# Two graph-attention layers on one core: the dense products beside the edge sums traced in four column pieces, and a bias added by VectorE

## The chip, the cores and the metric

The kernel runs on one NeuronCore of a Trainium2 chip. The metric is the device time of one execution in microseconds (us). TensorE (PE) multiplies matrices, VectorE (DVE) and ScalarE (ACT) work element by element, GpSimd (POOL) writes the descriptors of the gathers, SyncE (SP) issues most plain transfers, and 16 DMA engines move the data between the device memory and the core's SBUF. PSUM is the memory into which TensorE writes.

## The reference, cut to what matters

A graph has 3125 nodes of 768 features and 53125 edges, sorted by destination, self-loops among them. The node table passes a norm and a ReLU, then two attention layers, and `x` is added at the end:

```python
def gat_conv(x, edge_index, W, a_src, a_dst, bias, heads, out_ch, concat):
    ...
    xl = (x @ W).reshape(n, heads, out_ch)
    ...
    alpha = e / (s[dst] + 1e-16)
    msg = xl[src] * alpha[:, :, None]
    out = jax.ops.segment_sum(msg, dst, num_segments=n)
    ...
h = gat_conv(x, edge_index, W1, a_src1, a_dst1, b1, HEADS, HID, True)
h = layer_norm(h, g1, be1)
h = jax.nn.relu(h)
h = h + (h0 @ Wr1 + br1)
h1 = h
h = gat_conv(h, edge_index, W2, a_src2, a_dst2, b2, 1, OUT_DIM, False)
h = layer_norm(h, g2, be2)
h = h + (h1 @ Wr2 + br2)
```

Layer 1 has 4 heads of 256 columns (1024 in all), layer 2 one head of 768. Everything is in 32-bit floats. The dense products of the change are `h0 @ Wr1` (its late part), `h1 @ W2` and `h1 @ Wr2`.

## The kernel before, in words

The nodes are cut into 25 blocks of 128 (the last has 53). The edges of a block are laid out in 17 tiles of 128 slots (8 in the last block), so that a tile's edges lead to one or two quarters of the block, 32 nodes each. The function `in_order` does all the work; `any_order` is for other inputs and does not run here.

**Before the sums.** Up to about 503 us the kernel computes the norm, the table of layer 1 (`x @ W1`), the edge lists, the attention weights of layer 1, and `h0 @ Wr1` for about half of the blocks.

**The sums of layer 1** (`sums`, L639, called at L1184). For every block there are five rounds (`ROUNDS`) of three or four tiles. For each tile, GpSimd issues an indirect DMA (L698) that gathers 128 rows of 1024 floats of the table by the edges' sources into one of 13 buffers `g`. VectorE makes the weights `w` (L718, L719). TensorE then adds the products (L738): each takes 32 weight columns, one quarter's nodes, and writes 32 partitions of PSUM, so that four of them cover the four quarters of a block. After each round `step` lets the other work of TensorE advance, in an order that is written out by hand: the ends of earlier blocks, and `later`, which computes the late part of `h0 @ Wr1` (L1101) at the pace of the tuple `(2.5, 3.8, 0, 0, 0.9)` per round. The end of a block (`end1`, L1129) normalizes the sum, turns it by TensorE transposes (L1151), adds the residual (L1158, VectorE, both sources in SBUF), and multiplies by `W2` (L1173) to make a row block of layer 2's table, `table2`. That table must be whole before the first gather of layer 2.

**The sums of layer 2** (from L1187). The scheme is the same with rows of 784 floats and 36 buffers for the gathers (`RING`, issued by `fetch`, L1280). For each block, ScalarE copies the edge values (L1300), TensorE turns them (L1318), VectorE and ScalarE form the softmax (L1321 to L1328), TensorE turns the result back (L1332), and then come five rounds of sums (L1354). After each round, `filled` advances `residuals` (L1249), which computes `h1 @ Wr2` (L1259) some three blocks ahead: one of eight steps of K after each of the first four rounds, and four steps after the fifth. In round 2 the transposes L1318 stand between the sums and the product, in round 4 the transposes L1332. VectorE ends a block with L1367 (reads PSUM), L1370, the norm's statistics (L480, L482), L1373 and L1374.

**The biases `br2` and `be2`.** `split_biases` (L200) adds them, divides the sum into two rounded parts and stores them. `bias_rows` (L214) loads these as two rows. At the last step of K, two products of a row of ones with them (L1263) add them into PSUM:

```python
for k in range(NK2):
    for i, pm in enumerate(pms):
        nc.tensor.matmul(pm[:, :f], h1[:, k, :r], wr2[:, k, i * f:(i + 1) * f],
                         start=(k == 0), stop=False)
    if k == NK2 - 1:
        for i, pm in enumerate(pms):
            nc.tensor.matmul(pm[:, :f], ones_r[:, :r], ball_r[:, i * f:(i + 1) * f],
                             start=False, stop=True)
    yield
```

VectorE then adds the result to `xr`, a block of `x` (L1268). One 32-bit product in the program gives two matmul instructions and two weight loads in the trace.

Of the kernel before, what the change touches and what calls it, by code (L numbers as in the profile page):

```python
# [10 lines left out]
F32 = mybir.dt.float32  # L11
F32R = mybir.dt.float32r
# [5 lines left out]
OP = mybir.AluOpType  # L18
# [50 lines left out]
def in_order(  # L69
# [69 lines left out]
    hot_d = dram.tile([NB, 128, WIN], F8, name="hot_d")  # L139
    parts_d = dram.tile([2, C2], F32, name="parts_d")  # L140

# [3 lines left out]
    nc.vector.tensor_copy(ident_b, ident)  # L145
    ones_r = const.tile([2, P], F32R, name="ones_r")
    nc.vector.tensor_scalar(ones_r, ident[0:2, :P], 0.0, 1.0, op0=OP.mult, op1=OP.add)
    eps = const.tile([128, 1], F32, name="eps")
# [28 lines left out]
    def bcast(vec, n, parts=P):  # L177
        return bass.AP(tensor=vec.tensor, offset=vec.offset, ap=[[0, parts], [1, n]])

    def pieces(b):  # L180
        n = rows_of(b)
        m = n - n % 16
        return [(0, m), (m, n)] if m < n else [(0, n)]
# [15 lines left out]

    def split_biases(pool):  # L200

# [4 lines left out]
        nc.vector.tensor_add(v, v, u)  # L206
        hi = pool.tile([128, C2 // 128], F32R, name="ball_hi")
        nc.vector.tensor_copy(hi, v)
        lo = pool.tile([128, C2 // 128], F32R, name="ball_lo")
        nc.vector.tensor_sub(lo, v, hi.bitcast(F32))  # L210
        for i, t in enumerate((hi, lo)):
            nc.sync.dma_start(parts_d[i, :].rearrange("(p c) -> p c", p=128), t.bitcast(F32))

    def bias_rows(pool, name):  # L214
        t = pool.tile([2, C2], F32R, name=name)
        nc.sync.dma_start(t.bitcast(F32), parts_d)
        return t

# [535 lines left out]
    with tc.tile_pool(name="m1", bufs=1) as mp:  # L754
# [8 lines left out]
        with tc.tile_pool(name="h0", bufs=1) as hp, tc.tile_pool(name="pm1", bufs=1, space=PSUM) as pm1, \  # L763
# [9 lines left out]
            with tc.tile_pool(name="w1", bufs=1) as wp, tc.tile_pool(name="d1", bufs=2) as dp, \  # L773
# [216 lines left out]
                fill = early()  # L990
                split_biases(mp)
                for _ in products_:
# [82 lines left out]
        with tc.tile_pool(name="w2", bufs=1, reuse_waits="tile") as wp, tc.tile_pool(name="e1", bufs=2, reuse_waits="tile") as ep, \  # L1075
# [14 lines left out]
            def later():  # L1090
                for i, members in enumerate(late_in):
# [6 lines left out]
                    for m in range(NK2):  # L1098
                        pm = pp.tile([128, 512], F32, name="pr", bufs=2)
                        for k in range(NK1):  # L1100
                            nc.tensor.matmul(pm[:, :n], wr1[:, k, m * 128:(m + 1) * 128], loaded[i, k][:, :n],  # L1101
                                             start=(k == 0), stop=(k == NK1 - 1))
                            if m == NK2 - 1:
# [25 lines left out]
            def end1(b, z, share):  # L1129
# [41 lines left out]
                for k in range(NK2):  # L1171
                    for pm, (o, n) in zip(pms, halves):
                        nc.tensor.matmul(pm[:, :n], hT[:, k, :r], w2[:, k, o:o + n],  # L1173
                                         start=(k == 0), stop=(k == NK2 - 1))
                    if k in (2, 5, 7):
                        yield
# [10 lines left out]
    with tc.tile_pool(name="m2", bufs=1, reuse_waits="tile") as mp, \  # L1187
# [13 lines left out]
        for t in slots:  # L1201
            nc.vector.memset(t, 0.0)
        ball_r = bias_rows(mp, "ball_r")
        nc.vector.tensor_tensor(both, asad2[:, :, 0], asad2[:, :, 1], OP.add)
# [39 lines left out]
        owns = {0: small([128, C2], "own")}  # L1244
        z0 = small([P, C2], "z", bufs=2)
        nc.sync.dma_start(b2_b, bcast(b2, C2))
        nc.sync.dma_start(g2_b, bcast(g2, C2))

        def residuals():  # L1249

            for b in range(NB):
# [5 lines left out]
                for k in range(NK2):  # L1257
                    for i, pm in enumerate(pms):
                        nc.tensor.matmul(pm[:, :f], h1[:, k, :r], wr2[:, k, i * f:(i + 1) * f],  # L1259
                                         start=(k == 0), stop=False)  # L1260
                    if k == NK2 - 1:
                        for i, pm in enumerate(pms):
                            nc.tensor.matmul(pm[:, :f], ones_r[:, :r], ball_r[:, i * f:(i + 1) * f],  # L1263
                                             start=False, stop=True)
                    yield
# [635 lines left out]
```

## Time and profile before

| What | Value |
|---|---|
| Time, median of 3 runs | 1811.11 us (1810.21 to 1814.62) |
| The profiled execution's own time | 1811.92 us |
| Its span, first to last instruction | 1810.0 us |
| Mean granted TensorE clock | 0.974 |
| Busy: PE, DVE, ACT, POOL | 1691.0, 974.1, 452.4, 882.0 us |
| Gathers of layer 1 (L698), of layer 2 (L1287) | 416 and 416 |
| First and last sum of layer 1 (L738) | 503.5 and 1190.3 us |
| First and last gather issue of layer 2 | 1225.5 and 1775.6 us |

Times inside the trace count from the start of the span. "Busy" is the union of an engine's instructions. A row of a view that groups instructions gives the line, the engine, the operation, its output and inputs, the shape, how many there were, their busy time and the mean of one in ns, and the idle time just before them with what ended it. "DMA share" is the busy share of the 16 DMA engines, in which overlapping packets count twice, so that it can pass 1.

### The profile page before, as it was taken

The numbers are of one execution on the slowest core, as the hardware profiler recorded it, in microseconds if no ns is written. First come the engines' busy times: TensorE is split into PE (matmuls) and PEld (weight loads), VectorE is DVE, ScalarE is ACT, GpSimd is POOL, SyncE is SP. The second block draws the span as 40 slices with busy tenths as digits, with TensorE's granted clock in tenths as the row PEclk, the third lists the DMA queues.
The fourth block names the chain that finished last, engine by engine and source line by source line (L and its number), as shares of the span: only waits on it lengthen the run. The fifth ranks groups of instructions, "written<-read, shape, count | busy, mean of one in ns | idle before, by whom it ended". The sixth has DMA issues, their size and how long they took to land. (4 is left out here: it accounts for less than half of the span.)

```text
span 1810.0 us, 30659 instructions
## 1 busy us (share of the span) xinstructions
PE 1691.0 (93%) x11397; PEld 945.2 (52%) x11397; DVE 974.1 (54%) x2617; ACT 452.4 (25%) x1286; POOL 882.0 (49%) x922
## 2 busy tenths in 40 slices
PE   7999999899968999999999999996989999899995
PEld 5666665566535656566565455543434444344432
DVE  7683443788855465655656664631334444344445
ACT  2222331000121222122122112122333333343333
POOL 2000112000056566666666665606777777777772
PEclk9999999999988999999999999998999999999997
DMA  7834546533199999999999999939999999999994
GB/s 237 274 104 144 137 123 203 219 120 122 36 366 408 365 401 393 389 407 381 404 410 402 411 398 372 385 128 358 343 381 383 395 386 372 380 390 392 377 358 152
DMA packets 173674, 561.37 MB, mean 310 GB/s; under 512 B 28740, under 2 KB 54106, under 8 KB 173388
## 3 DMA queue, kind: packets, MB, share of 16 engines
q0 software_dynamic: 100912, 402.06, 58.2%
q1 hardware_dynamic: 68210, 146.87, 22.7%
q10 hardware_dynamic: 4394, 10.39, 1.5%
q8 instruction: 93, 1.52, 0.3%
q14 instruction: 65, 0.53, 0.1%
HBM read 498.23 MB, written 65.62 MB: 312 GB/s over the span
## 5 line engine op out<-in xcount | busy, mean ns | idle before, releaser
L698 POOL DMA_INDIRECT g<-table,idx_s x416 | 408.0, 981 | 418.1 <-DVE m L619 175.5
L1287 POOL DMA_INDIRECT g<-table,idx_s x416 | 417.8, 1004 | 179.5 <-issue 62.3
L1259 PE MATMUL pr<-wr,h 128*128 128x384 f32 (+1 forms) x800 | 293.1, 508 | 0.0
L738 PE MATMUL pa<-g,w 128*32 128x256 f32 x3912 | 261.0, 390 | 23.6 <-DMA g<-table,idx_s 12.5
L1173 PE MATMUL p<-w,h1T 128*128 128x384 f32 (+2 forms) x800 | 279.8, 498 | 2.6 <-DVE h1T L1158 2.6
L1259 PEld LDWEIGHTS pr<-wr,h 128*128 128x128 f32 (+1 forms) x800 | 145.0, 193 | 123.5 <-issue 53.3
L1173 PEld LDWEIGHTS p<-w,h1T 128*128 128x128 f32 (+1 forms) x800 | 144.9, 188 | 122.2 <-issue 25.2
L738 PEld LDWEIGHTS pa<-g,w 128*32 128x32 f32 x3912 | 125.2, 111 | 152.4 <-issue 30.1
L1354 PE MATMUL pa<-g,w 128*32 128x384 f32 x1956 | 192.7, 507 | 3.1 <-DVE v L1379 3.1
L719 DVE TENSOR_TENSOR w<-oh,al 128x128 f32<-128x128 f32 (+1 forms) x416 | 131.9, 317 | 91.3 <-PE pa L738 57.0
L1321 DVE CUSTOM_DVE_ANT_0 e<-mix,pen 128x640 f32<-128x640 f32 x25 | 20.6, 825 | 235.1 <-PE mix L1318 235.1
L1101 PE MATMUL pr<-h0k,wr 128*128 128x256 f32 (+1 forms) x576 | 141.0, 392 | 0.0
L843 PE MATMUL pm<-w,h0l 128*128 128x344 f32 (+1 forms) x468 | 140.8, 455 | 0.0
L980 PE MATMUL pm<-h0g,wr 128*128 128x512 f32 x288 | 132.0, 606 | 0.0
L843 PE MATMUL pm<-w,h0g 128*128 128x344 f32 x432 | 130.8, 459 | 0.3 <-ACT h0g L822 0.3
L1300 ACT ACTIVATE slots<-g 128x32 f32<-128x32 f32 x416 | 73.7, 221 | 221.7 <-DMA g<-table,idx_s 221.6
L1101 PEld LDWEIGHTS pr<-h0k,wr 128*128 128x128 f32 x576 | 106.9, 191 | 29.4 <-issue 9.0
L911 POOL DMA_DIRECT2D hot_d<-ohd x25 | 13.4, 537 | 219.0 <-DVE own L497 121.5
L1354 PEld LDWEIGHTS pa<-g,w 128*32 128x32 f32 x1956 | 54.5, 112 | 117.7 <-issue 91.4
L718 DVE TENSOR_SCALAR oh<-iota_f,rel_s 128x32 f32<-128x32 f32 (+1 forms) x416 | 110.1, 265 | 0.1
L843 PEld LDWEIGHTS pm<-w,h0l 128*128 128x128 f32 (+1 forms) x468 | 84.9, 186 | 44.0 <-issue 5.7
L843 PEld LDWEIGHTS pm<-w,h0g 128*128 128x128 f32 x432 | 82.0, 193 | 40.6 <-issue 1.6
(286 smaller groups left out, 1640.7 us busy)
## 6 DMA issues: line engine op xcount, KB each, us to landing
s<-slo_d SPq DMA_DIRECT2D x25, 544.0 KB
g<-table,idx_s POOLq DMA_INDIRECT x832
table<-row SPq DMA_DIRECT2D x24, 512.0 KB
own<-table SPq DMA_DIRECT2D x24, 512.0 KB
h1T_d<-h1T SPq DMA_DIRECT2D x24, 512.0 KB
h<-h1T_d SPq DMA_DIRECT2D x22, 512.0 KB
table<-row SPq DMA_DIRECT2D x24, 392.0 KB
ring<-in_x_dram SPq DMA_DIRECT2D x24, 384.0 KB
```

Source lines behind the costliest of these rows:

```text
L698: nc.gpsimd.indirect_dma_start(out=g, out_offset=None, in_=table[:, :], in_offset=bass.IndirectOffsetOnAxis(ap=idx_s[:, b * J + j:b * J + ...
L718: nc.vector.tensor_scalar(oh, iota_f[:, lo:hi], rel_s[:, c:c + 1], None, op0=OP.is_equal)
L719: nc.vector.tensor_tensor(w, oh[:, None, :].to_broadcast([128, heads, hi - lo]), al[:, POS[j], :, b:b + 1].to_broadcast([128, heads, hi - ...
L738: nc.tensor.matmul(pa[32 * q:32 * q + 32, o // f, o % f:o % f + n], w[:, o // cols, :], g[:, o:o + n], start=to not in opened, stop=False, ...
L843: nc.tensor.matmul(pm[:r, :C], h0[b][:, k, :], w1[:, k, i * C:(i + 1) * C], start=(k == 0), stop=(k == NK1 - 1))
L980: nc.tensor.matmul(pm, wr1[:, k, m * 128:(m + 1) * 128], groups[gi][:, k, :], start=(k == 0), stop=(k == NK1 - 1))
L1101: nc.tensor.matmul(pm[:, :n], wr1[:, k, m * 128:(m + 1) * 128], loaded[i, k][:, :n], start=(k == 0), stop=(k == NK1 - 1))
L1173: nc.tensor.matmul(pm[:, :n], hT[:, k, :r], w2[:, k, o:o + n], start=(k == 0), stop=(k == NK2 - 1))
L1259: nc.tensor.matmul(pm[:, :f], h1[:, k, :r], wr2[:, k, i * f:(i + 1) * f], start=(k == 0), stop=False)
L1287: nc.gpsimd.indirect_dma_start(out=g, out_offset=None, in_=table2[:, :], in_offset=bass.IndirectOffsetOnAxis(ap=idx_s[:, b * J + j:b * J + ...
L1300: nc.scalar.activation(slots[b % 2][:, POS[j], :], gs[b, j][:, C2:C2 + 1].to_broadcast([128, 32]), AF.Copy)
L1354: nc.tensor.matmul(pa[32 * q:32 * q + 32, i, :f], w_, g[:, i * f:(i + 1) * f], start=(i, q) not in opened, stop=False, skip_group_check=True)
```

## The change

A helper `by_columns` splits a product's weights into pieces of at most 32 columns, each with the PSUM partitions of its own. The three dense products that run beside the sums (L1101, L1173, L1259) go through it, so that each becomes four products of 32 weight columns over the same moving data. The row of ones, the two rounded parts and the two products L1263 go. In their place `br2 + be2` is stored whole, loaded once into all 128 partitions (`ball_b`, by SP, just ahead of `b2_b`), and VectorE adds it to each block's `xr` at step 5 of K.

```diff
--- before.py
+++ after.py
@@ -137,14 +137,12 @@
     slo16_d = dram.tile([NB * S], I16, name="slo16_d")
     keep_d = dram.tile([H * NB, S + 2], BF16, name="keep_d")
     hot_d = dram.tile([NB, 128, WIN], F8, name="hot_d")
-    parts_d = dram.tile([2, C2], F32, name="parts_d")
+    ball_d = dram.tile([C2], F32, name="ball_d")
 
     ident = const.tile([128, 128], F32, name="ident")
     make_identity(nc, ident)
     ident_b = const.tile([128, 128], BF16, name="ident_b")
     nc.vector.tensor_copy(ident_b, ident)
-    ones_r = const.tile([2, P], F32R, name="ones_r")
-    nc.vector.tensor_scalar(ones_r, ident[0:2, :P], 0.0, 1.0, op0=OP.mult, op1=OP.add)
     eps = const.tile([128, 1], F32, name="eps")
     nc.vector.memset(eps, EPS)
     iota_i = const.tile([128, 128], I32, name="iota_i")
@@ -177,6 +175,12 @@
     def bcast(vec, n, parts=P):
         return bass.AP(tensor=vec.tensor, offset=vec.offset, ap=[[0, parts], [1, n]])
 
+    def by_columns(out_, lhsT, rhs, m, start, stop):
+
+        for o in range(0, m, 32):
+            e = min(o + 32, m)
+            nc.tensor.matmul(out_[o:e], lhsT[:, o:e], rhs, start=start, stop=stop, skip_group_check=True)
+
     def pieces(b):
         n = rows_of(b)
         m = n - n % 16
@@ -197,24 +201,14 @@
         nc.sync.dma_start(t, vec.rearrange("(k p) -> p k", p=128))
         return t
 
-    def split_biases(pool):
+    def sum_biases(pool):
 
         v = pool.tile([128, C2 // 128], F32, name="ball_v")
         nc.sync.dma_start(v, br2.rearrange("(p c) -> p c", p=128))
         u = pool.tile([128, C2 // 128], F32, name="ball_u")
         nc.sync.dma_start(u, be2.rearrange("(p c) -> p c", p=128))
         nc.vector.tensor_add(v, v, u)
-        hi = pool.tile([128, C2 // 128], F32R, name="ball_hi")
-        nc.vector.tensor_copy(hi, v)
-        lo = pool.tile([128, C2 // 128], F32R, name="ball_lo")
-        nc.vector.tensor_sub(lo, v, hi.bitcast(F32))
-        for i, t in enumerate((hi, lo)):
-            nc.sync.dma_start(parts_d[i, :].rearrange("(p c) -> p c", p=128), t.bitcast(F32))
-
-    def bias_rows(pool, name):
-        t = pool.tile([2, C2], F32R, name=name)
-        nc.sync.dma_start(t.bitcast(F32), parts_d)
-        return t
+        nc.sync.dma_start(ball_d.rearrange("(p c) -> p c", p=128), v)
 
     def divided(pool, v, shape, name, by=P):
 
@@ -988,7 +982,7 @@
                                 yield
 
                 fill = early()
-                split_biases(mp)
+                sum_biases(mp)
                 for _ in products_:
                     pass
                 for _ in range(6):
@@ -1098,8 +1092,8 @@
                     for m in range(NK2):
                         pm = pp.tile([128, 512], F32, name="pr", bufs=2)
                         for k in range(NK1):
-                            nc.tensor.matmul(pm[:, :n], wr1[:, k, m * 128:(m + 1) * 128], loaded[i, k][:, :n],
-                                             start=(k == 0), stop=(k == NK1 - 1))
+                            by_columns(pm[:, :n], wr1[:, k, m * 128:(m + 1) * 128], loaded[i, k][:, :n], 128,
+                                       start=(k == 0), stop=(k == NK1 - 1))
                             if m == NK2 - 1:
                                 load(i + 1, k)
                             if k == NK1 - 1:
@@ -1170,8 +1164,8 @@
                 pms = [pp.tile([128, 512], F32, name="p2", bufs=2)[:r] for _ in range(2)]
                 for k in range(NK2):
                     for pm, (o, n) in zip(pms, halves):
-                        nc.tensor.matmul(pm[:, :n], hT[:, k, :r], w2[:, k, o:o + n],
-                                         start=(k == 0), stop=(k == NK2 - 1))
+                        by_columns(pm[:, :n], hT[:, k, :], w2[:, k, o:o + n], r,
+                                   start=(k == 0), stop=(k == NK2 - 1))
                     if k in (2, 5, 7):
                         yield
                 for pm, (o, n) in zip(pms, halves):
@@ -1200,7 +1194,7 @@
         slots = [small([128, J, 32], f"slots{i}") for i in range(2)]
         for t in slots:
             nc.vector.memset(t, 0.0)
-        ball_r = bias_rows(mp, "ball_r")
+        ball_b = small([P, C2], "ball_b")
         nc.vector.tensor_tensor(both, asad2[:, :, 0], asad2[:, :, 1], OP.add)
         nc.vector.scalar_tensor_tensor(self_s, both, SLOPE, both, op0=OP.mult, op1=OP.max)
         hots, pens = {}, {}
@@ -1243,6 +1237,7 @@
             rows[(i + J) % RING] = small([128, RW], f"g{(i + J) % RING}")
         owns = {0: small([128, C2], "own")}
         z0 = small([P, C2], "z", bufs=2)
+        nc.sync.dma_start(ball_b, bcast(ball_d, C2))
         nc.sync.dma_start(b2_b, bcast(b2, C2))
         nc.sync.dma_start(g2_b, bcast(g2, C2))
 
@@ -1256,12 +1251,10 @@
                 pms = [pp.tile([P, 512], F32, name=f"pr{i}", bufs=2)[:r] for i in range(2)]
                 for k in range(NK2):
                     for i, pm in enumerate(pms):
-                        nc.tensor.matmul(pm[:, :f], h1[:, k, :r], wr2[:, k, i * f:(i + 1) * f],
-                                         start=(k == 0), stop=False)
-                    if k == NK2 - 1:
-                        for i, pm in enumerate(pms):
-                            nc.tensor.matmul(pm[:, :f], ones_r[:, :r], ball_r[:, i * f:(i + 1) * f],
-                                             start=False, stop=True)
+                        by_columns(pm[:, :f], h1[:, k, :], wr2[:, k, i * f:(i + 1) * f], r,
+                                   start=(k == 0), stop=(k == NK2 - 1))
+                    if k == 5:
+                        nc.vector.tensor_add(xr[:r], xr[:r], ball_b[:r])
                     yield
                 for i, pm in enumerate(pms):
                     cs = slice(i * f, (i + 1) * f)
```

## The prediction, made before the result was known

> **What bounds the kernel now.** I read the busy times by stage first, then the chain of waits where layer 2 begins, then GpSimd's gathers.
>
> ```profile
> core 0: us, PE busy (x) PEld busy (x) DVE busy (x) ACT busy (x) POOL busy (x), PEclk, DMA share, GB/s
> 503.00:620.00 117.00, 100.36 (x827) 60.91 (x827) 59.15 (x192) 20.53 (x52) 66.32 (x66) 0.91 1.00 386
> 620.00:1180.00 560.00, 553.12 (x4567) 321.79 (x4564) 333.56 (x1124) 110.30 (x315) 355.98 (x372) 1.00 1.01 397
> 985.00:1050.00 65.00, 59.36 (x524) 31.73 (x523) 42.53 (x144) 13.06 (x35) 42.96 (x45) 1.00 1.03 411
> 1100.00:1140.00 40.00, 40.00 (x330) 22.59 (x332) 24.79 (x83) 10.14 (x31) 25.17 (x28) 1.00 0.95 350
> 1225.00:1260.00 35.00, 20.06 (x65) 11.67 (x64) 1.02 (x2) 6.58 (x20) 23.27 (x25) 0.83 1.00 375
> 1260.00:1777.00 517.00, 477.31 (x2854) 213.67 (x2852) 211.99 (x458) 197.39 (x601) 394.23 (x392) 0.96 1.00 377
> ```
>
> Layer 1 (620 to 1180) has two limits close together. TensorE is busy 553.12 of 560 us, and the DMA engines carry a share of 1.01. Where TensorE idles most (985 to 1050, 59.36 of 65 us) the share is 1.03: that is what full DMA engines look like here. Where TensorE never idles (1100 to 1140) the share falls to 0.95, because GpSimd waits for buffers that the sums free.
>
> ```profile
> L698 POOL DMA_INDIRECT g<-table,idx_s x416: 932/937/4222, 307.0 to 1168.6; - x139
> ...
>   PE pa L738: 114.3, 83
> ...
> L1287 POOL DMA_INDIRECT g<-table,idx_s x416: 940/946/1742, 1225.5 to 1775.6; - x139
> ...
>   issue: 62.3, 201
> ...
>   PE pa L1354: 7.4, 23
> ```
>
> In layer 1 GpSimd waits 114.3 us for the sums. In layer 2 it waits for nothing: a gather takes 0.946 us at the median, and the 0.30 us between two (7.4 us over 23 times, 62.3 over 201) stands before nearly every one, whatever is named. 416 x (0.946 + 0.30) = 518 us of the 550 from the first to the last issue. Layer 2 is **GpSimd's row of gathers**, and TensorE, with 40 us idle in 517, follows it.
>
> **What the change takes off TensorE.**
>
> ```profile
> 1267.87 0.55 PE mix L1332 x5
> 1268.42 5.16 PE pr L1259 x16
> 1273.58 0.54 PE pr L1263 x2
> 1274.12 1.43 PE pa L1354 x16
> 1275.55 1.49 PE pr L1259 x4
> ...
> 1282.07 1.29 PE pr L1259 x4
> ...
> 1287.71 0.70 PE mix L1332 x5
> ```
>
> Sixteen dense instructions take 5.16 us, 0.3225 each, so four take 1.29, and they do so behind transposes (1282.07); behind a sum they take 1.49. Sixteen sum instructions, side by side in fours, would take 4 x 0.3225 = 1.29 too, and take 1.43 behind a product. A trip from sums to a product and back thus costs 0.20 + 0.14 = **0.34 us**, which goes when the product has the sums' form. Behind transposes nothing goes: the product now pays the 0.14 that the next sum paid, and transposes behind a sum (0.70) or a product (0.55) change places.
>
> ```profile
> 528.80 1.89 PE L738 MATMUL pa<-g,w 128*32 128x256 f32 x26 [1.06 <-DMA g<-table,idx_s]
> 530.61 1.56 PE L1101 MATMUL pr<-h0k,wr 128*128 128x256 f32 x6
> ...
> 1189.01 1.92 PE L738 MATMUL pa<-g,w 128*32 128x256 f32 x16
> 1190.86 1.56 PE L1173 MATMUL p<-w,h1T 128*128 128x384 f32 x4
> ```
>
> Layer 1 has 91 such trips in the timeline (first and last above): 31 us. Layer 2 has three a block in the 22 blocks whose rounds carry a product: 66, 22 us. L1263 goes, 25 x 0.54 = 13.5 us. Together 67 us of TensorE's time.
>
> That a dense product in four pieces runs as fast as a whole one no row shows. Nearest are the sums: by the 1.29 above, equal. By busy time L738 (261.0 us for 3912, so 0.267 for four) stands against L1101 (141.0 for 576, 0.245), 9% more, but its row holds the very trips that go. I take equal; 9% on the 421 us of L1101 and L1173 would put back 38 us and undo layer 1's gain.
>
> ```profile
> L1259 PE MATMUL pr<-wr,h 128*128 128x384 f32 (+1 forms) x800 | 293.1, 508 | 0.0
> L1173 PE MATMUL p<-w,h1T 128*128 128x384 f32 (+2 forms) x800 | 279.8, 498 | 2.6 <-DVE h1T L1158 2.6
> L738 PE MATMUL pa<-g,w 128*32 128x256 f32 x3912 | 261.0, 390 | 23.6 <-DMA g<-table,idx_s 12.5 <-DVE w L719 4.4 <-DVE oh L718 4.0
> L1101 PE MATMUL pr<-h0k,wr 128*128 128x256 f32 (+1 forms) x576 | 141.0, 392 | 0.0
> q8 instruction: 93, 1.52, 0.3%
> ```
>
> **Layer 1: what of 31 us reaches the end.** With TensorE 1.2 us a block faster, the DMA engines are the next limit. They have 560 x (1 - 1.01/1.03) = 11 us to give (19 by the bytes, 397 against 411 GB/s). A heavy block as at 1100 still outlasts its transfers, so I take 6. Instructions are fetched too: 1.52 MB now for some 22,800 of TensorE's; layer 1 adds 3 x 1376 matmuls with as many loads, 0.55 MB, 1.4 us at 397 GB/s. Behind the last gather, where TensorE alone sets the end, two or three trips go: 0.7 us. Sum for layer 1: **-6 + 1.4 - 0.7 = -5.3 us** (bounds: -16 and 0).
>
> **Layer 2: the 36 us on TensorE buy nothing**; they lengthen its wait before L1318. What counts is what the added VectorE instruction does to GpSimd.
>
> ```profile
> 1464.62 1.02 DVE L1374 SCALAR_TENSOR_TENSOR z<-z,bn_rs,xr 128x768 f32<-128x768 f32 x1
> ...
> 1474.17 1.02 DVE L1268 TENSOR_TENSOR xr<-pr,xr 128x384 f32<-128x384 f32 x2 [1.69 <-PE pr L1263]
> ```
> ```profile
> 1464.76 1.70 POOL L1287 DMA_INDIRECT g<-table,idx_s  x1 [0.30 <-ACT v L1328]
> ...
> 1474.81 0.95 POOL L1287 DMA_INDIRECT g<-table,idx_s  x1 [0.31 <-ACT slots L1300]
> ```
> ```profile
> 1102.63 0.69 DVE L1158 TENSOR_TENSOR h1T<-h1T,r1l 128x512 f32<-128x512 f32 x1 [4.65 <-ACT h1T L1156]
> ```
> ```profile
> 1102.86 1.27 POOL L698 DMA_INDIRECT g<-table,idx_s  x1 [0.30 <-issue]
> ```
>
> A gather that starts while VectorE reads two SBUF operands (L1374, and L1158, a plain addition) ends some 0.82 us after VectorE does: it takes 1.70 and 1.27 instead of 0.94. Beside L1268, which reads PSUM, it takes its 0.95. The new addition reads `xr` and `ball_b`, both in SBUF.
>
> ```profile
> L1374 DVE SCALAR_TENSOR_TENSOR z<-z,bn_rs,xr 128x768 f32<-128x768 f32 x24 | 24.9, 1038 | 0.8
> L1373 DVE SCALAR_TENSOR_TENSOR z<-z,bn_mv,g_b 128x768 f32<-128x768 f32 x24 | 24.0, 999 | 0.0
> L1370 DVE SCALAR_TENSOR_TENSOR z<-z,v,b_b 128x768 f32<-128x768 f32 x24 | 24.0, 999 | 0.0
> L1325 DVE SCALAR_TENSOR_TENSOR e<-e 128x640 f32<-128x640 f32 x25 | 20.4, 818 | 0.0
> L1287 POOL DMA_INDIRECT g<-table,idx_s x416 | 417.8, 1004 | 179.5 <-issue 62.3 <-DMA ball_r<-parts_d 45.5 <-ACT slots L1300 26.8
> ```
>
> The four that there are hold VectorE 93 us and the gathers 417.8 - 416 x 0.946 = 24 us: 0.26 per us. The new one takes about 0.96 us (0.69 for 512 columns, so 0.0013 a column more) and runs 23 times beside gathers that nothing else limits: 0.26 x 0.96 x 23 = 5.7 us. It stands straight ahead of L1370, and a gather held by the first of two often slips past the second, so I take 5. Bounds: 0, and 0.75 each (1.70 - 0.95), 17 us. VectorE itself has room (212 of 517 us). On the queue of SP the 6 KB of `ball_r` become 384 KB of `ball_b` ahead of `b2_b`, while the first gathers fill the DMA engines (share 1.00 at 375 GB/s from 1225 on): **1 us** later.
>
> The Trainium skill ("SBUF — State Buffer", Who interferes with whom) says that two SBUF inputs contend with GpSimd's reads, but infers that tensor_tensor does not hold up the writing of descriptors. By that the addition would cost 0 and the sum be 4 us lower; L1158 beside the 1.27 us gather speaks against it.
>
> **Sum.** On the profiled execution's 1811.92 us: -5.3 + 5 + 1 = +0.7. Against the median of the runs, 1811.11, it stands 0.8 higher, so I give the sum there: **1812**, no difference that can be measured (0.3%, 5.4 us, is about what a measurement here can tell).
>
> **Rivals.**
> - **The DMA engines give all they have** and the addition falls between gathers: -11 from 620 to 1180, -3 from 503 to 620 (share 1.00 of 1.03), -0.7, +1.4, +1, +2: -10, 1801. For it: the queue is deep wherever the share is 1.03. Against it: TensorE's heavy blocks. 0.23.
> - **Slower: the addition locks onto the gathers.** If it is mostly under way when a gather starts, each costs up to 0.75 us: +17, and 1811 - 5 + 1 + 17 = 1824. It decides above some 0.5 us a block. For it: VectorE then reads SBUF twice for 2 us on end, longer than a gather's 1.25 us cycle. Against it: the 0.26 mean. 0.22.
> - **A plain addition does not hold gathers**, a rule weighed above: 1811 - 5.3 + 1 = 1807. 0.06, since L1158's row shows one that does.
> - **TensorE sets both layers** after all, and all 67 us come through: 1744. Against it: 1.03 and the row of gathers. 0.03.
> - **The pieces do not run side by side**, so the change does not do what it says: 714 us of dense busy time would at least double, 2500. The sums' own calls have the same form. 0.03.
>
> **Chances.** The forecast has 0.43. Faster by over 0.3%: 0.23 + 0.03 = 0.26. Within: 0.43 + 0.06 = 0.49. Slower: 0.22 + 0.03 = 0.25. The range runs from 1799 (the first rival and 2 us) to 1825 (the second and 1 us) and leaves the ends of these and the last two out, some 0.15; the forecast's own is 1806 to 1817.
>
> **What would show it.** The chain in layer 2 without the 1.49 and 1.43, but 1.29 each; no L1263. TensorE's busy time some 67 us lower at about the same span, idle before L1318 and before the sums L738. DMA share 1.02 or more from 620 to 1180, and the last sum of layer 1 some 5 us before 1190. From the first to the last issue of layer 2's gathers 556 us instead of 550, the median still 0.946 and the mean above 1.004. The forecast is wrong if GpSimd shows waits for `pa` in layer 2, or if a product's four pieces take longer than the whole.

## The result, and the profile after

The changed kernel takes 1805.37 us (median of 13 runs, 1801.14 to 1809.85) against 1813.43 us before (13 runs, 1810.21 to 1817.84): ratio 0.9956, 95% interval 0.9943 to 0.9968. It is faster by 8 us, 0.44%. I had forecast no measurable difference, 1812 us. The profiled executions differ by 10.8 us (span 1810.0 to 1799.2), and three instructions split that: the first gather of layer 2 starts at 1211.09 for 1225.49 (**-14.4**), the row of gathers to the last one takes 553.8 us for 550.1 (**+3.7**), and what follows the last gather is the same.

The timeline of GpSimd after, first and last gather of layer 2 (start, us, engine, line):

```profile
1211.09 1.00 POOL L1280 DMA_INDIRECT g<-table,idx_s  x1 [45.13 <-DMA hot<-hot_d]
...
1764.93 1.73 POOL L1280 DMA_INDIRECT g<-table,idx_s  x1 [0.30 <-ACT e L1320]
```

The busy times by stage, after; the last two columns are the DMA share and GB/s.

```profile
core 0: us, PE busy (x) PEld busy (x) DVE busy (x) ACT busy (x) POOL busy (x), PEclk, DMA share, GB/s
503.00:620.00 117.00, 98.93 (x1350) 57.82 (x1354) 60.20 (x195) 20.76 (x52) 68.94 (x68) 0.87 1.01 393
620.00:1180.00 560.00, 545.21 (x8036) 297.61 (x8028) 341.24 (x1139) 111.53 (x318) 353.50 (x370) 1.00 1.01 401
620.00:1150.00 530.00, 515.37 (x7699) 281.41 (x7695) 326.79 (x1096) 106.02 (x303) 344.94 (x357) 1.00 1.02 405
985.00:1050.00 65.00, 59.64 (x812) 36.49 (x816) 42.52 (x143) 9.48 (x26) 42.09 (x44) 1.00 1.03 411
1100.00:1140.00 40.00, 40.00 (x596) 20.11 (x592) 26.47 (x88) 8.45 (x25) 27.82 (x29) 1.00 1.02 390
1245.60:1762.60 517.00, 445.57 (x4929) 179.77 (x4931) 229.69 (x475) 196.54 (x596) 394.77 (x390) 0.95 1.00 376
```

The same stretch of before, cut at 1150 because the gathers of after end near there:

```profile
620.00:1150.00 530.00, 524.13 (x4316) 306.03 (x4315) 315.53 (x1065) 102.89 (x296) 336.22 (x348) 1.00 1.01 396
```

From 620 to 1150 the DMA engines move 405 GB/s for 396, and the heavy stretch from 1100 to 1140, in which TensorE still never idles, goes from a share of 0.95 and 350 GB/s to 1.02 and 390. The last row is the stretch of layer 2 that the prediction showed (1260 to 1777), 14.4 us earlier, as its gathers are. It moves no faster (376 GB/s for 377), while TensorE idles 71 us of 517 there, for 40 before.

GpSimd's waits after:

```profile
POOL g L692 <- PE pa L732: 59.2, 63, 6.4
POOL g L692 <- DMA g<-table,idx_s: 58.1, 66, 3.5
POOL g L1280 <- DMA hot<-hot_d: 45.1, 1, 45.1
POOL g L1280 <- ACT slots L1293: 25.1, 77, 1.4
...
POOL g L1280 <- PE pa L1347: 6.2, 18, 1.0
```

In layer 1 GpSimd waited 114.3 us for the sums; now 59.2 for the sums and 58.1 for landed gathers. That is the second limit coming up beside the first. In layer 2 it waits for `pa` no more than before (6.2 for 7.4).

The chain of waits after, in layer 2:

```profile
1287.07 1.43 PE pr L182 x16
1288.50 1.29 PE pa L1347 x16
1289.79 1.29 PE pr L182 x16
```

As forecast, a product behind transposes now pays the 0.14 us (1.43), and between sums and products nothing is paid any more (1.29 each).

### The profile page after: what moved, and what is told of

It is laid out like the page before. It is cut to its first block, busy times and chain, and to the rows that moved or that the text cites. A ratio compares the mean times of both kernels' runs of the same rounds, so it can differ in the third digit from the quotient of the medians.

```text
span 1799.2 us, 43360 instructions
## 1 busy us (share of the span) xinstructions
PE 1637.3 (91%) x17747; PEld 870.2 (48%) x17747; DVE 998.1 (55%) x2639; ACT 454.1 (25%) x1286; POOL 885.9 (49%) x922
## 3 DMA queue, kind: packets, MB, share of 16 engines
q0 software_dynamic: 100912, 402.06, 58.1%
q8 instruction: 142, 2.33, 0.5%
## 5 line engine op out<-in xcount | busy, mean ns | idle before, releaser
L1280 POOL DMA_INDIRECT g<-table,idx_s x416 | 421.5, 1013 | 179.2 <-issue 63.7
L732 PE MATMUL pa<-g,w 128*32 128x256 f32 x3912 | 276.5, 389 | 32.0 <-DMA g<-table,idx_s 21.1
L182 PE MATMUL pr<-wr,h 128*32 128x384 f32 (+1 forms) x3136 | 292.4, 504 | 0.0
L182 PE MATMUL p<-w,h1T 128*32 128x384 f32 (+1 forms) x3136 | 283.9, 489 | 2.6 <-DVE h1T L1152 2.6
L732 PEld LDWEIGHTS pa<-g,w 128*32 128x32 f32 x3912 | 144.6, 112 | 146.1 <-issue 28.7
L1347 PE MATMUL pa<-g,w 128*32 128x384 f32 x1956 | 196.3, 509 | 3.1 <-DVE v L1372 3.1
L182 PEld LDWEIGHTS p<-w,h1T 128*32 128x32 f32 x3136 | 123.1, 110 | 125.6 <-issue 85.8
L713 DVE TENSOR_TENSOR w<-oh,al 128x128 f32<-128x128 f32 (+1 forms) x416 | 132.0, 317 | 80.4 <-PE pa L732 45.5
L182 PEld LDWEIGHTS pr<-wr,h 128*32 128x32 f32 (+1 forms) x3136 | 100.6, 112 | 151.0 <-issue 150.1
L182 PE MATMUL pr<-h0k,wr 128*32 128x256 f32 (+1 forms) x2304 | 146.9, 391 | 0.9 <-DMA h0k<-h0T_d 0.9
L1347 PEld LDWEIGHTS pa<-g,w 128*32 128x32 f32 x1956 | 67.9, 116 | 110.5 <-issue 97.7
L182 PEld LDWEIGHTS pr<-h0k,wr 128*32 128x32 f32 x2304 | 80.5, 111 | 55.0 <-issue 9.2
L1311 PE MATMUL mix<-ident,slots 128*128 128x128 f32 x125 | 22.5, 319 | 88.1 <-ACT slots L1293 88.1
```

Source lines behind the costliest of these rows:

```text
L182: nc.tensor.matmul(out_[o:e], lhsT[:, o:e], rhs, start=start, stop=stop, skip_group_check=True)
L713: nc.vector.tensor_tensor(w, oh[:, None, :].to_broadcast([128, heads, hi - lo]), al[:, POS[j], :, b:b + 1].to_broadcast([128, heads, hi - ...
L732: nc.tensor.matmul(pa[32 * q:32 * q + 32, o // f, o % f:o % f + n], w[:, o // cols, :], g[:, o:o + n], start=to not in opened, stop=False, ...
L1280: nc.gpsimd.indirect_dma_start(out=g, out_offset=None, in_=table2[:, :], in_offset=bass.IndirectOffsetOnAxis(ap=idx_s[:, b * J + j:b * J + ...
L1311: nc.tensor.transpose(mix[:, c * 128:(c + 1) * 128], at[:, o:o + 4].rearrange("p q n -> p (q n)"), ident)
L1347: nc.tensor.matmul(pa[32 * q:32 * q + 32, i, :f], w_, g[:, i * f:(i + 1) * f], start=(i, q) not in opened, stop=False, skip_group_check=True)
```

## The experiments

The theory: all of the gain is layer 1's, where TensorE fell behind the DMA engines as the next limit; layer 2 is GpSimd's row of gathers, the pieces buy nothing there, and the addition costs some 4 us by holding up gathers. The experiments ran on four chips; each ratio is to the kernel before on the same chip. On one of them (e5 to e8) the kernel before took 1945.8 us and the engines waited for things that the profile does not name, so those four are read apart, at the end.

| run | ratio to before, 95% | first gather of layer 1 to first of layer 2 | row of layer 2's gathers | their busy time |
|---|---|---|---|---|
| before | 1 | 918.4 us | 550.1 us | 417.8 us |
| the change | 0.9956 (0.9943 to 0.9968) | 903.5 | 553.8 | 421.5 |
| e1 layer 1 in pieces | 0.9924 (0.9902 to 0.9946) | 907.1 | 549.1 | 418.2 |
| e2 layer 2 in pieces, addition | 1.0017 (0.9999 to 1.0034) | 919.0 | 551.9 | 420.3 |
| e3 addition alone | 1.0025 (1.0009 to 1.0042) | 919.2 | 549.8 | 421.4 |
| e4 all in pieces, no addition | 0.9930 (0.9908 to 0.9953) | 904.8 | 550.2 | 412.6 |
| e9 before, TensorE's work cut | 0.9932 (0.9915 to 0.9950) | 906.8 | 550.4 | 416.3 |
| e10 three more additions | 1.0089 (1.0071 to 1.0106) | 904.4 | 578.8 | 449.5 |
| e11 three one-operand passes | 0.9986 (0.9973 to 0.9999) | 904.7 | 561.5 | 429.9 |
| e12 the change again | 0.9968 (0.9956 to 0.9980) | 902.9 | 554.6 | 420.4 |
| e13 layer 1 in pieces again | 0.9936 (0.9925 to 0.9948) | 905.5 | 551.8 | 418.6 |

The three last columns are from one profiled execution each; starts in the timeline give the first two. Layer 1's column falls into two sets, 918.4 to 919.2 and 902.9 to 907.1, with nothing between.

**The parts, one by one: e1 to e4.** e1 is the kernel before with this alone:

```diff
-                            nc.tensor.matmul(pm[:, :n], wr1[:, k, m * 128:(m + 1) * 128], loaded[i, k][:, :n],
-                                             start=(k == 0), stop=(k == NK1 - 1))
+                            by_columns(pm[:, :n], wr1[:, k, m * 128:(m + 1) * 128], loaded[i, k][:, :n], 128,
+                                       start=(k == 0), stop=(k == NK1 - 1))
...
-                        nc.tensor.matmul(pm[:, :n], hT[:, k, :r], w2[:, k, o:o + n],
-                                         start=(k == 0), stop=(k == NK2 - 1))
+                        by_columns(pm[:, :n], hT[:, k, :], w2[:, k, o:o + n], r,
+                                   start=(k == 0), stop=(k == NK2 - 1))
```

> Only the two products of layer 1 (L1101 and L1173 of the kernel before) in four pieces; layer 2 as before, biases by L1263. Theory (all of the gain is layer 1's, where TensorE fell behind the DMA engines; the addition costs layer 2 some 4 us): the last sum of layer 1 starts near 1176 as after, the row of layer 2's gathers takes 550 us as before, the time is 14 us lower than before, ratio 0.992, and so below the changed kernel. Rival 1 (layer 2's pieces bring part of the 8 us): the time is 5 to 8 us lower than before at most, ratio 0.996 or more.

e2 is the changed kernel with these two products whole again.

> Layer 1 as before; layer 2's product in four pieces and br2 + be2 added to x by VectorE. Theory: TensorE gets some 35 us less to do in layer 2 and nothing of it shows; the addition holds up gathers, so the row of layer 2's gathers takes 554 us for 550 and the time is 4 us higher than before, ratio 1.002. Rival 1 (layer 2's pieces bring something): ratio 0.998 or less. Rival 2 (the addition is harmless and the 3.7 us are something else): 1.000 if they came with layer 1's pieces, 1.002 if they come with layer 2's.

e3 is e2 with layer 2's product whole as well, so that only the biases' way differs from before:

```diff
-                        by_columns(pm[:, :f], h1[:, k, :], wr2[:, k, i * f:(i + 1) * f], r,
-                                   start=(k == 0), stop=(k == NK2 - 1))
+                        nc.tensor.matmul(pm[:, :f], h1[:, k, :r], wr2[:, k, i * f:(i + 1) * f],
+                                   start=(k == 0), stop=(k == NK2 - 1))
```

> All products whole as before; only the biases move, from L1263's products to VectorE's addition. Theory: the row of layer 2's gathers takes 554 us for 550, ratio 1.002, the same as with layer 2's pieces beside it. Rival 2 (the 3.7 us come with the pieces, their 2400 more instructions or the other rhythm of TensorE, not with the addition): the row stays at 550, ratio 1.000.

e4 is e1 with layer 2's product in pieces too, and the biases still by the products of the ones:

```diff
-                        nc.tensor.matmul(pm[:, :f], h1[:, k, :r], wr2[:, k, i * f:(i + 1) * f],
+                        by_columns(pm[:, :f], h1[:, k, :], wr2[:, k, i * f:(i + 1) * f], r,
                                          start=(k == 0), stop=False)
```

> All three products in pieces as in the changed kernel, but the biases still added by TensorE (L1263's whole products of the ones). Theory: layer 1 gives its 14 us, the row of gathers is back at 550, ratio 0.992, as with layer 1's pieces alone and some 4 us below the changed kernel. Rival 2 (the pieces, not the addition, lengthen the row of gathers): ratio 0.994 to 0.996, as the changed kernel.

e1 gives 0.9924 and e4 0.9930: layer 1 alone brings 13 us, and layer 2's pieces nothing that their intervals of 4 us to each side can show. e2 and e3 stand at 1.0017 and 1.0025, so layer 2's part of the change is a loss of some 3 to 5 us, with pieces or without; e3's interval is clear of 1, e2's touches it. All four came out as the theory had it in time, though e4's interval alone (to 0.9953) would also hold its rival's 0.994. In the traces two things did not. The last sum of layer 1 starts at 1183.4 us in e1, not near 1176 (its first gather is 2.3 us later than before, and layer 1 gains 11.3 us). And e3's row of gathers is 549.8 us and not 554, though its gathers are busy 421.4 us; the gaps between them came out shorter in that execution. A single profile carries an effect of 4 us badly (e4's gathers happen to be busy 412.6), so its size needed a dose and a pair on one chip.

**Is layer 1's floor the DMA engines? e9.** The kernel before, products whole and trips kept, leaves out four of the six k-steps of L1101, so that layer 1's residual product is incomplete; every load stays. It has 94 us less for TensorE (384 of the 576 instructions at 0.245 us), three times what the change removes in layer 1.

```diff
                         for k in range(NK1):
-                            nc.tensor.matmul(pm[:, :n], wr1[:, k, m * 128:(m + 1) * 128], loaded[i, k][:, :n],
+                            if k in (0, NK1 - 1):
+                                nc.tensor.matmul(pm[:, :n], wr1[:, k, m * 128:(m + 1) * 128], loaded[i, k][:, :n],
```

> The kernel before without four of the six k-steps of each L1101 product once more, because the chip of the first time ran the kernel before itself in 1946 us, with TensorE waiting at issue. If this chip runs the kernel before near 1812, theory (the DMA engines' floor stops the gain, and pieces are only one way to bring TensorE under it): layer 1 from the first gather to the last sum takes 861 to 868 us for 883 of the kernel before, ratio 0.990. Rival 1 (TensorE sets layer 1): 50 us or more under it, 0.972. Rival 2 (the DMA engines had only the 6 us that the share of 1.03 allows, the rest came of the pieces themselves): 0.997.

Its first gather of each layer, its last group of sums in layer 1, the stage from 620 to 1150, and TensorE's wait for gathers:

```profile
308.90 1.01 POOL L698 DMA_INDIRECT g<-table,idx_s  x1 [2.02 <-PE pm L980]
...
1215.69 1.00 POOL L1288 DMA_INDIRECT g<-table,idx_s  x1 [44.68 <-DMA hot<-hot_d]
```
```profile
1179.30 1.92 PE L738 MATMUL pa<-g,w 128*32 128x256 f32 x16
```
```profile
620.00:1150.00 530.00, 499.25 (x4155) 266.69 (x4154) 332.19 (x1119) 106.03 (x304) 351.28 (x362) 1.00 1.03 408
```
```profile
PE pa L738 <- DMA g<-table,idx_s: 50.5, 42, 18.1
```
```profile
554.57 0.95 POOL L684 DMA_INDIRECT ao<-alo_d,at_last  x1 [21.09 <-DMA alo_d<-scr]
```

It is 0.9932, and layer 1 takes 906.8 us: as long as with the pieces. TensorE now waits 50.5 us for gathers (12.5 in the kernel before), and the share is 1.03. So the pieces are only one way to take TensorE out of the way, and something else stops the gain. Rival 1 (50 us and more) and rival 2 (6 us) both fall. By the mark I had set (861 to 868 us to the last sum) it was 2 us late: 1179.30 - 308.90 = 870.4 us to its last group of sums.

That the two times agree so closely is in part luck. GpSimd stands 21.1 us in e9 before one small gather of attention values (the last line above; 6.6 us in the kernel before), so at its 61st gather e9 is 17.6 us behind the kernel before, and only then does it gain. The rates are the better measure: from 620 to 1150 e9 moves 408 GB/s and the change 405, so the change has some 4 us left above e9's rate (530 x (1 - 405/408), an estimate). No run changed the transfers themselves; that they are the floor is read from this rate, which comes near the best stretch's 411, and from TensorE's wait for gathers.

**What the addition costs: e10 to e13.** e10 puts three more instructions of the addition's form into each block of the changed kernel (the maximum of xr and xr, which changes no value); e11 the same three with one operand.

```diff
+                    if k in (1, 3, 7):
+                        nc.vector.tensor_tensor(xr[:r], xr[:r], xr[:r], OP.max)
                     if k == 5:
                         nc.vector.tensor_add(xr[:r], xr[:r], ball_b[:r])
```
```diff
+                    if k in (1, 3, 7):
+                        nc.vector.tensor_scalar(xr[:r], xr[:r], 0.0, None, op0=OP.add)
```

> The changed kernel with three more two-operand instructions a block, once more for the same reason. If this chip runs the kernel before near 1812, theory (each holds up gathers by 3.7 us in all): gathers' busy time in layer 2 some 433 us, the row some 565, 11 us over the changed kernel, ratio 1.002. Rival (the 3.7 us were the phase): 421, 552 to 554 and 0.9956. On the first chip the gathers' busy time was 428.7 with the three and 418.7 with three of one operand.

> The changed kernel with three more VectorE instructions a block that read one SBUF operand (xr plus zero, 768 columns). Theory (the second SBUF operand holds the gathers; three more two-operand ones made the gathers' busy time 449.5 us and the ratio 1.0089): gathers' busy time 418 to 424 us, ratio 0.995 to 0.997, as the changed kernel. Rival (any VectorE work on SBUF holds them): busy time 430 us or more, ratio 1.000 or more.

e12 is the changed kernel itself and e13 is e1, on the same chip as e11.

> The changed kernel itself, on the same chip as the two beside it. If the chip runs the kernel before near 1812: ratio 0.9956, 8 us under it. If it is one on which TensorE waits at issue: slower than before by 5% or more, because four times the instructions must be delivered.

> Layer 1's products in pieces, layer 2 as before, on the same chip as the changed kernel. Theory (the addition costs what one two-operand instruction a block costs): 4 to 8 us under the changed kernel, ratio to before 0.992. Rival (the addition is hidden): as the changed kernel, 0.995 to 0.996.

The groups of gathers and of the instructions in question, in after, e10 and e11 (busy us, mean ns of one):

```profile
L1280 POOL DMA_INDIRECT g<-table,idx_s x416 | 421.5, 1013 | 179.2 <-issue 63.7 <-DMA hot<-hot_d 45.1 <-ACT slots L1293 25.1
...
L1257 DVE TENSOR_TENSOR xr<-xr,ball_b 128x768 f32<-128x768 f32 (+1 forms) x25 | 23.7, 946 | 16.3 <-DMA xr<-in_x_dram 10.4 <-DMA ball_b<-ball_d 5.9
```
```profile
L1282 POOL DMA_INDIRECT g<-table,idx_s x416 | 449.5, 1080 | 173.3 <-issue 61.3 <-DMA hot<-hot_d 43.0 <-ACT slots L1295 25.8
...
L1257 DVE TENSOR_TENSOR xr<-xr 128x768 f32<-128x768 f32 (+1 forms) x75 | 71.4, 952 | 12.6 <-DMA xr<-in_x_dram 11.6
```
```profile
L1282 POOL DMA_INDIRECT g<-table,idx_s x416 | 429.9, 1033 | 178.1 <-issue 68.0 <-DMA hot<-hot_d 45.6 <-ACT slots L1295 25.5
...
L1257 DVE TENSOR_SCALAR xr<-xr 128x768 f32<-128x768 f32 (+1 forms) x75 | 41.9, 559 | 12.7 <-DMA xr<-in_x_dram 11.8
```

The 75 two-operand instructions lengthen the gathers by 28.0 us and the kernel by some 24 (0.0133 of 1811): more than the linear 11 that I expected: 8 us for one such instruction a block, and 28.0/71.4 = 0.39 us of gathers per us of VectorE, where the prediction had 0.26. That they hold up gathers, and that layer 2's time follows the gathers, is thereby shown. It shows in the single gathers too: of the 42 in e10 that start 0.2 us or more before the end of one of the new instructions, 41 end 0.81 to 0.83 us after that end. e13 is 0.9936 where e12 is 0.9968: layer 2's part of the change, of which the addition is the only thing that can be seen to hold up anything, costs 0.0032, **6 us**, and layer 1's pieces bring 12 to 14. With e2 and e3 beside it, the cost is 3 to 6 us; in the profiled executions the row of gathers is 2.8 us longer in e12 than in e13, and 3.7 in the change than before.

e11 refutes the other half of my expectation, though it stays just short of its rival's marks (430 us and 1.000). One operand is not free: 8.4 us of longer gathers (0.20 per us of VectorE), a row of 561.5 us for 554.6 in e12, and 0.9986 instead of 0.9968. The timeline of VectorE and of GpSimd in e11:

```profile
1503.44 0.68 DVE L1330 COPY w<-mix 128x512 f32<-128x512 f32 x1
...
1509.10 0.55 DVE L1257 TENSOR_SCALAR xr<-xr 128x768 f32<-128x768 f32 x1
```
```profile
1503.53 0.94 POOL L1282 DMA_INDIRECT g<-table,idx_s  x1 [0.30 <-issue]
...
1509.38 1.09 POOL L1282 DMA_INDIRECT g<-table,idx_s  x1 [0.30 <-ACT slots L1295]
```

The gather beside L1257 ends at 1510.47, 0.82 us after VectorE's 1509.65: the same hold as beside two operands, and 37 of the 39 gathers that start 0.2 us or more before the end of such an instruction show it (0.81 to 0.83 us). The one beside L1330, which reads PSUM, takes its 0.94. It is the shorter instruction (0.559 us for 768 columns, against 0.952) that costs less, not the missing operand. An estimate from these rows: a gather that would take 0.946 us and ends 0.82 us after VectorE is held by what is left of the instruction at its start, less 0.13 us. If starts fall at random in the 1.25 us from one gather to the next, an instruction of 0.952 us costs 0.27 us and one of 0.559 us 0.075, so 75 of them cost 20 and 5.6 us, a ratio of 3.6; 28.0 and 8.4 were measured, a ratio of 3.3. By this estimate the cost grows with about the square of the instruction's time.

Not every instruction with one operand in SBUF holds a gather. The norm's statistics read `z` there; in the kernel before, VectorE and GpSimd:

```profile
1311.97 1.02 DVE L480 BATCH_NORM_STATS2 bn_st<-z 128x6 f32<-128x384 f32 x2
...
1312.08 0.95 POOL L1287 DMA_INDIRECT g<-table,idx_s  x1 [0.30 <-ACT slots L1300]
```

None of the 21 gathers that start beside these statistics takes more than 0.95 us.

The Trainium skill ("SBUF — State Buffer", Who interferes with whom) says that tensor_scalar from SBUF to SBUF can enter a mode that takes both of VectorE's ports and then excludes GpSimd; 0.559 us against 0.952 and the held gather (e11's L1257) agree with that. Its inference that tensor_tensor does not hold up the writing of descriptors is refuted by e10's 28.0 us.

**The four on the disturbed chip: e5 to e8.** e5 is e10's kernel, e8 e11's, e7 e9's; e6 is the changed kernel with e9's cut.

> The changed kernel with three more VectorE instructions a block of the addition's form (two operands in SBUF, 768 columns: the maximum of xr and xr, which leaves the values as they are), at three other places of the block. Theory (each such instruction holds up gathers): four where there was one, so the gathers' busy time in layer 2 grows by three times 3.7 us, to some 433, the row from the first to the last issue to some 565, and the time is 11 us over the changed kernel's, ratio to before some 1.002. Bound from the prediction's rival (0.75 us a block and instruction): 52 us over. Rival (the 3.7 us of the one profile were the chance of the phase, and the addition is harmless): 421 us, row 552 to 554, ratio 0.9956 as the changed kernel.

> The changed kernel without four of the six k-steps of each L1101 product (the sums of layer 1's residual product are then incomplete; all loads stay): about 94 us of TensorE's work less in layer 1. Theory (after the change layer 1 is bound by the DMA engines, with some 4 us of slack left between blocks 3 and 24): layer 1 from the first gather to the last sum shrinks by 2 to 8 us from 869, no more. Rival (TensorE still sets layer 1): it shrinks by 50 us or more.

> The kernel before (all products whole) without the same four of six k-steps: 94 us of TensorE's work less, and the trips between product and sums kept. Theory (the DMA engines' floor is what stops the gain, and pieces are only one way to bring TensorE under it): layer 1 from the first gather to the last sum takes as long as in the changed kernel with the same left out, 861 to 867 us for 883 of the kernel before, time some 18 us under it, ratio 0.990. Rival 1 (TensorE sets layer 1): 50 us or more under it. Rival 2 (the DMA engines had only the 6 us that the share of 1.03 allows, and the other 8 came of the pieces themselves): 6 us under it, ratio 0.997.

> The same three places, but an instruction with one operand in SBUF (xr plus zero). Theory (it is the second SBUF operand that holds the gathers): gathers' busy time stays near 421 us, the ratio near the changed kernel's 0.9956. Rival (any VectorE work on SBUF beside the gathers lengthens them, in proportion to its time): between this and the run with the two operands.

Their ratios are 1.087, 1.056, 0.999 and 1.086 to a kernel before of 1945.8 us, so none meets in time what any theory said. In e5 and e8 the gathers' busy times, 428.7 and 418.7 us, looked like a difference between two operands and one; their rows take 703 and 701 us there, so the gathers stand farther apart, and e11 did not bear it out. None of the four is taken as evidence on layers 1 and 2. What TensorE waited for in e7 and in e5, and VectorE's longest wait in e7:

```profile
PE pa L1355 <- issue: 45.0, 68, 1.6
PE pa L738 <- issue: 42.1, 74, 1.1
...
PE mix L1319 <- issue: 17.2, 6, 13.4
```
```profile
PE pr L182 <- issue: 106.1, 182, 2.1
PE pa L732 <- issue: 38.6, 79, 1.0
PE pa L1349 <- issue: 15.8, 27, 2.0
```
```profile
DVE e L1322 <- remote: 241.4, 18, 37.2
```

"issue" is time in which the engine waited for nothing that the profile shows. e7 has 126 us of it on TensorE; the same kernel on another chip (e9) has 0.9. "remote" is a wait whose end the profile cannot put down to anything on this core; it stands in these four runs and neither in before nor in e9. Most of the longer time does not show as waiting on TensorE at all: its busy time is 1872.2 us in e5 and 1649.2 in e10, the same kernel. The three kernels in pieces were 5.6 to 8.7% slower than before there, e6 among them, although it has 94 us less to do than the change. That their many more instructions are what costs so much on such a chip would fit the place of the waits in e5 (L182, the pieces), but it is not shown: what delayed the issue is not in the profile, and the changed kernel itself did not run there. That stays open. e6's question, whether the change with less of TensorE's work gets any faster, was not asked again on another chip; the some 4 us by e9's rate are the nearest answer.

**A version that beats both** is e1, layer 1's pieces alone: 0.9924 and, on another chip, 0.9936, 6 us under the changed kernel beside it.

## Why the prediction was wrong, step by step

- **What bounds the kernel: right.** Two limits close together in layer 1, GpSimd's row in layer 2. e9 shows that TensorE alone does not set layer 1, e10 and e4 show GpSimd's row.
- **The trips, 0.34 us each: right in form.** The chain shows 1.29 and 1.43 as drawn. TensorE's busy time fell by 54 us (1691.0 to 1637.3) and not 67. Layer 1's sums are busy 276.5 us where they had 261.0, but that row can't be read so: the busy times of TensorE's groups add up to 1760.8 us before and 1774.0 after, far more than TensorE was busy, because groups overlap. If each instruction counts only from the end of those that started before it, layer 1's sums go from 252.8 to 243.1 us, the three products from 689.5 to 670.8, layer 2's sums from 184.7 to 172.5, and L1263's 13.5 go. The trips thus gave 41 us of the 53 forecast. In e1 and e13, with a granted clock of 0.973 and 0.976 (0.974 before), layer 1's pieces take 23 and 28 us of their 31 off TensorE; in the change the clock is 0.965. Whether the lower clock is the rest is not shown.
- **Four pieces run as fast as a whole product: right.** The groups of the three products and of layer 1's sums after:

```profile
L182 PE MATMUL pr<-wr,h 128*32 128x384 f32 (+1 forms) x3136 | 292.4, 504 | 0.0
L182 PE MATMUL p<-w,h1T 128*32 128x384 f32 (+1 forms) x3136 | 283.9, 489 | 2.6 <-DVE h1T L1152 2.6
L732 PE MATMUL pa<-g,w 128*32 128x256 f32 x3912 | 276.5, 389 | 32.0 <-DMA g<-table,idx_s 21.1 <-DVE w L713 4.2 <-DVE oh L712 3.1
...
L182 PE MATMUL pr<-h0k,wr 128*32 128x256 f32 (+1 forms) x2304 | 146.9, 391 | 0.9 <-DMA h0k<-h0T_d 0.9
```

  The three products take 723.2 us together, against 713.9 whole: 1.3% more, not the 9% that I bounded, and less than whole by the count without overlaps.
- **Layer 1, "-6 of 11": the step that failed.** The mechanism held, its size did not: -5.3 was forecast, and -14.4 came to the first gather of layer 2. I had two estimates of what the DMA engines could still give, 11 us by the share (1.01 of 1.03) and 19 by the bytes (397 of 411 GB/s), took the smaller and then half of it, on the ground that a heavy block as at 1100 outlasts its transfers. That ground was wrong. The 361st and the last of layer 1's 416 gathers, before and after:

```profile
1079.08 0.94 POOL L698 DMA_INDIRECT g<-table,idx_s  x1 [0.30 <-issue]
...
1168.59 0.94 POOL L698 DMA_INDIRECT g<-table,idx_s  x1 [0.30 <-issue]
```
```profile
1070.43 0.93 POOL L692 DMA_INDIRECT g<-table,idx_s  x1 [0.30 <-issue]
...
1153.60 1.01 POOL L692 DMA_INDIRECT g<-table,idx_s  x1 [0.30 <-issue]
```

  The change is 8.65 us ahead at the one and 15.0 at the other: the heavy end, which that ground had left out, brought 6.3 us, and the stretch at 1100 went from 350 to 390 GB/s. The other 9 us came between some 600 and 1079; the 61st gather, near 590, starts 0.5 us later than before. So the stage gave 15.5 us, between the 11 of the share and the 19 of the bytes.
  The share was too small because it counts the time of packets, and this time is not a constant: the stretch at 1100 had a share of 0.95 at 350 GB/s before, 8% more for each GB/s than 1.03 at 411. The page's lines of the queue that carries the gathers, before and after:

```profile
q0 software_dynamic: 100912, 402.06, 58.2%
```
```profile
q0 software_dynamic: 100912, 402.06, 58.1%
```

  The same packets and bytes took 58.2% of 1810.0 us of each DMA engine before and 58.1% of 1799.2 after. Summed packet by packet, that is 1052.7 and 1046.2 us: 6.5 us less, which a share of 1.01 had shown as work. In e10, whose gathers of layer 2 are held longest, the same packets took 1059.5. The Trainium skill ("Perfetto Trace Analysis", Identifying the Most-Contended Engine) calls the DMA engines' occupancy misleading and asks for the bandwidth in its place; the packets' times here agree that the occupancy misleads, though the bytes by themselves promised 3.5 us more than came.
- **Instructions fetched, +1.4:** the instruction queue carries 2.33 MB for 1.52, and 2.03 in e13, so layer 1's part is 0.51 MB (0.55 forecast). Its time cannot be told apart.
- **Layer 2, the 36 us on TensorE buy nothing: right** (e4 against e1).
- **The addition, +5: right.** 3 to 6 us by the runs, 3.7 of longer gathers in the profile. The gathers that start beside it are lengthened by 6.1 us in the change, 6.3 in e12 and 4.6 in e3; the net is smaller, 2.6 to 3.7, since other holds fall away. One figure of the working was a slip that did no harm: 0.69 us and 0.0013 for each of 256 more columns make 1.02 us, not 0.96, and 0.946 was measured. And if the addition cost nothing, the sum would be 5 us lower, not 4. The 8 us of each further instruction show that the bound of 17 was not idle.
- **The load of `ball_b`, +1: not seen.** GpSimd's wait before the first gather of layer 2 is 45.1 us after and 45.5 before.
- **The rivals.** "The DMA engines give all they have" had the right sum for layer 1, -14, but partly by luck: of its -3 before 620 nothing came, and the stage behind gave 15.5 for its 11. Its term for the addition, +2, was too small. The measured time lies between it and the forecast: -14.4 with its size, +3.7 with the forecast's. "A plain addition does not hold gathers" falls with e10. The slower rival, 0.75 us a block, was too dear: 3.7 us over 23 blocks is 0.16 us each, and even the three further ones come to 28.0/75 = 0.37. TensorE does not set both layers (e9), and the pieces do run side by side.

With the bytes' 19 us and no halving, the sum would have been -19 + 1.4 - 0.7 + 5 + 1 = -12; with the 14 that the rival took, -7. The profiled executions differ by -10.8, the medians by -8.

## What to carry to other kernels

Where two engines are close to their limits, what the second one can still give decides what relief of the first is worth; take the busy share and the bytes per second, each against the best stretch of the same stage, as two bounds (11 and 19 us here, 15.5 came), and do not halve them for a stretch that looks bound by the first engine: that stretch gained the most for its length. Count switches between forms of matmul by their places: the same trip was worth time in one layer and none in the other. And do not move work to VectorE beside a row of indirect gathers if the engine that it leaves has time to spare: the products of the ones cost nothing here that the runs can show, the addition 3 to 6 us.

## What the runs showed of the hardware that I had not expected

- A one-operand `tensor_scalar` from SBUF to SBUF (0.559 us for 768 columns) holds a gather as the two-operand instruction does, to 0.82 us after VectorE's end; 75 of them cost 8.4 us, 75 two-operand ones 28.0. The norm's statistics, with one operand in SBUF too, hold none (21 gathers, at most 0.95 us).
- The same packets and bytes of the gathers' queue took 1052.7 us of each DMA engine before, 1046.2 after and 1059.5 in e10: their time goes with the pace of the kernel. A busy share near 1 thus does not by itself say that the DMA engines are full: layer 2 has 1.00 at 376 GB/s, where GpSimd sets the pace, and layer 1 1.03 at 411.
- One and the same kernel took 1800.4 us on one chip and 1943.2 on another, with 0.9 and 126 us of TensorE's time waiting at issue, and 1636.9 and 1713.6 us of it busy.
